# Attention with bias, a gated feed-forward and two adapters: three turned heads in even groups, Gelus of two half batches together, fewer transfers through DRAM copies

## The chip, the core and the metric

The kernel runs on one core of a Trainium2 chip. A core has a matrix engine (TensorE, "PE" in the profile; its weight loads are listed apart as "PEld"), a vector engine (VectorE, DVE), a scalar engine for activation functions (ScalarE, ACT), a general engine (GpSimd, POOL), and SyncE (SP), whose queue issues the transfers of this kernel. Sixteen DMA engines carry the transfers out. On-chip data lie in 128 partitions; TensorE writes to eight PSUM banks.

The metric is device time in microseconds (us) of one execution, as the median of several. The kernel before takes 891.4 us (three runs, 889.95 to 893.95).

## The reference, cut to what matters

Eight batch entries of 512 tokens by 256 features pass an attention block with 16 heads of 16 features and a bias for every head, query and key (8 x 16 x 512 x 512 floats, 134 MB), then a feed-forward block, an adapter whose inner matrix is chosen by a token per batch entry, a rotation, and a second adapter of the same form.

```python
emb = silu(_sin_emb(timestep)) @ W_ada + b_ada
scale, shift = split(emb[:, None, :], 2)
x = _ln(src) * (1.0 + scale) + shift
q, k, v = heads(x @ Wq + bq), heads(x @ Wk + bk), heads(x @ Wv + bv)
scores = einsum('bhqd,bhkd->bhqk', q / sqrt(16), k) + attention_bias
probs = softmax(where(src_mask, -inf, scores))
x = x + (einsum('bhqk,bhkd->bhqd', probs, v) @ Wo + bo)
h = _ln(x) * g2 + beta2
x = x + _gelu2(h @ W1 + b1) @ W2 + b2          # _gelu2(x) = x * sigmoid(1.702 x)
# adapter, twice (before and after the rotation of groups of four features)
hidden = gelu(x @ down_W.T + down_b)
hidden = hidden @ expert_W[idx].T + expert_b[idx] + domain_emb[idx]
x = _ln(hidden @ up_W.T + up_b + x) * ln_gamma + ln_beta
```

## The kernel before

**Steps.** The attention of a batch entry is cut into 16 steps: two halves of 256 queries, four groups g of four heads, and in each two query tiles of 128 (i = 0 and 1). There are 128 steps in all, numbered n. In `attention`, a step loads four bias tiles of 128 x 512 (line 918), one per head j; POOL adds the mask (922); PE computes the four score tiles (930); DVE adds scores to bias and keeps the row's extreme (942); ACT takes the exponential (946). The probabilities then lie with queries on the partitions and have to be turned so that keys do. There are two ways to do that:

- Heads from `turned` on: PE transposes four blocks of 128 x 128 into a PSUM bank (981), and ACT or DVE copies the bank into the tile `pT` (`evict`, 702).
- Heads below `turned`: DVE transposes blocks of 32 x 32 into the tile `tb` (957), and four DMAs, on SP's queue, carry the blocks to their places in `pT` (966). These heads use the values in another order of rows, `v_turn`, which `prepare` makes out of `v_pad` by four DMAs (876).

`turned` is `TURNED = 2` in every group, but in batch 0 in its last group alone. After the second tile of a group come the value products (1007), a small transpose, the division by the sum of the row (1020 to 1036).

**Around it.** `prepare(b)` loads and normalises the next batch entry and makes queries, keys and values; its work is spread over the steps of the batch before. `finish(b, ts)` follows each half batch: output projection (`token_tiles`, 768), `feed_forward` (1061, 1070, 1073, 1077, 1086), then `adapter` twice, l = 0 and 1, then the store of the result (1196). `adapter` transposes the tokens (744, 702), multiplies by the down weight (1116), takes the Gelu on ACT (1124), multiplies by the expert's product with the up weight (768), adds (1133) and normalises. ACT holds one set of functions at a time: between the exponential (946) and the Gelu (1124) the profile shows ACT_TABLE_LOAD.

**At the start.** `late_weights` loads the weights that are needed after the first steps; `wo`, the output weight, comes in eight DMAs, as the host's array has 16 empty rows in each 32 (582). `experts_matrices` fetches, for each batch entry, the chosen expert's matrix of both adapters: SP reads the index into a register and issues two DMAs (1227, 1231).

**What sets the order.** Every piece of work is a task with the engine, a cost in us, what it reads and writes, and a rank. `Plan.run` runs through a model of the engines with these costs, and takes on each engine the ready task of lowest rank whose buffers are free (`Slots`: 15 bias tiles, three `tb`, two `pT`, four `res`, four PSUM banks for scores and four for the rest). `Plan.end` spreads the ranks of a stream (`finish` from n + 2 to n + 11); `Plan.stir` adds small random amounts to ranks, from a list of seeds. The result is a fixed order of instructions per engine; each engine and SP's queue run it in order and wait by semaphores. A transfer waits at SP for its buffer; everything behind it on SP waits too.

Of the kernel before, what the change touches and what calls it, by code (L numbers as in the profile page):

```python
# [20 lines left out]
P = 128  # L21
B, S, D, H, HD, FF = 8, 512, 256, 16, 16, 1024
NT = S // P
# [7 lines left out]
TURNED = 2  # L31
# [49 lines left out]
class Plan:  # L81
# [3 lines left out]
    AFTER = {PE: 0.22, DVE: 0.14, ACT: 0.16, POOL: 0.12, DMA: 2.2}  # L85
# [70 lines left out]
    def run(self, free_at):  # L156
# [13 lines left out]
        landed = [self.BACKLOG + 1.5] * self.FLIGHT  # L170
        while events:
# [15 lines left out]
            for e in [e for e in free_at if e in idle]:  # L187
# [33 lines left out]
                if e == DMA:  # L221
                    begun = now
                    for _ in range(t.many):
                        begun = max(begun, landed[-self.FLIGHT]) + cost / t.many
                        queues = max(queues, begun) + t.data / t.many
                        landed.append(queues + 1.5)
# [22 lines left out]
def conditioned_sequence_kernel(  # L249
# [24 lines left out]
    small = ctx.enter_context(tc.tile_pool(name="small", bufs=1))  # L274
# [8 lines left out]
    def slots(name, count, shape, dtype=F32):  # L283
        return Slots([const.tile(shape, dtype, tag=f"{name}{i}", name=f"{name}{i}") for i in range(count)])

# [13 lines left out]
    BIAS = slots("bias", 15, [P, S])  # L299
    LOW = slots("low", 4, [P, 4])  # L300
    PT = slots("pT", 2, [P, 4 * NT * 2 * P])
    TB = slots("tb", 3, [P, TURNED * S])
# [9 lines left out]
    ST = slots("st", 4, [P, 6])  # L312
    MV = slots("mv", 4, [P, NT, 2])
    RSTD = slots("rstd", 3, [P, 2, NT])
    MINUS = slots("minus", 2, [P, NT])
# [64 lines left out]
    def turned_groups(b):  # L380

        return (NG - 1 if b == 0 else 0), NG
# [23 lines left out]
    turned_rows = tc.dram_tile([B, D], F32, name="turned_rows")  # L406

    def embedding():

        tokf = small.tile([1, 2 * B], F32, tag="tokf", name="tokf")  # L410
        red = small.tile([P, B + 2], F32, tag="red", name="red")
        clip = small.tile([A, B], F32, tag="clip", name="clip")
# [8 lines left out]
        for i in range(42):  # L421
# [4 lines left out]
        plan(DVE, 0.2, lambda: nc.vector.tensor_copy(tokf, tok_i), [], ["tokf"], at=3.2)  # L426
        plan(PE, 0.3, lambda: nc.tensor.matmul(
            scr.t[:, 0, : 2 * B], ones, tokf, start=True, stop=True), ["tokf"], [scr],
            mode="full")

        def reduced():
            turns, last = scr.t[:, 2, : B + 2], scr.t[:, 3, : B + 2]
            nc.vector.tensor_scalar(
# [9 lines left out]
        plan(DVE, 1.2, reduced, [], [scr], at=4.0)  # L443
# [17 lines left out]
        def chosen():  # L461
            domf = scr.t[:A, 0, B : 2 * B]
# [5 lines left out]
        plan(DVE, 0.6, chosen, [], [scr, "valid", "expert"])  # L468
# [101 lines left out]
    def late_weights():  # L570
        wo_rows = w_o.rearrange("(c u j e) n -> c j u e n", c=NC, u=2, e=32)

        def load(rank, cost, data, emit, key, many=1):
# [7 lines left out]
        load(3.0, 3.6, 1.0, lambda: [  # L581
            nc.sync.dma_start(wo[32 * j : 32 * j + 32, c], wo_rows[c, j, :, :HD])
# [840 lines left out]
```

## Time and profile before

| What | us |
|---|---|
| median of three runs | 891.4 (889.95 to 893.95) |
| the profiled execution, its own time | 890.14 |
| its span on the core | 888.4 |
| PE busy | 860.4 (97%) |
| DVE busy | 783.0 (88%) |
| POOL busy | 775.3 (87%) |
| ACT busy | 740.7 (83%) |
| DMA, mean over 16 engines | 78.0% of the span, 217.22 MB on SP's queue |
| TensorE's granted clock, mean | 0.989 |

The page names, for each group of instructions, the line, the engine, the operation, the tiles, the shape and the count; after the bar the busy time in us and the mean ns of one, and after the next bar the idle time of the engine just before these instructions, with what ended most of it. "PE" rows are matmuls, "PEld" rows weight loads. A table by stretches gives each engine's busy time between two moments, counted from the start of the span, then the granted clock (1.00 is full speed), the share of the DMA engines and GB/s. In the list of waits a row reads: who, at which line, waited for which work, in total, how often, and the longest.

### The profile page before, as it was taken

To read this page: it belongs to the slowest core of one execution; us is meant where nothing else is said; L and a number is where in the kernel's file an instruction comes from. 1 tells how busy PE (TensorE), PEld (TensorE's weight loads), DVE (VectorE), ACT (ScalarE), POOL (GpSimd) and SP (SyncE) were. 2 spreads that over 40 slices of the span, in tenths; PEclk is the share of its full clock that TensorE was granted. 3 is DMA by queue.
4 is the path that set the end of the run, shared out by engine and by line. 5 is a ranking of instruction groups with operands and counts; after the bars stand their busy time and mean duration, and the time that the engine had idled before them with its cause. 6 is when DMAs were issued, how large, how long until landed. Compare 5 with 4: busy or idle time off the path is not lost.

```text
span 888.4 us, 20406 instructions
## 1 busy us (share of the span) xinstructions
PE 860.4 (97%) x6430; PEld 565.8 (64%) x6430; DVE 783.0 (88%) x2141; ACT 740.7 (83%) x1349; POOL 775.3 (87%) x907
## 2 busy tenths in 40 slices
PE   9998999999999999999999999999999999999994
PEld 7654675666666666656666666666666566666683
DVE  4757799989999999988998999899999999999766
ACT  5974779979898998979988897988979789799653
POOL 8867999999899898999889997998899999999432
PEclk9998999999999999999999999999999999999997
DMA  9577887698986988888896978968897898998400
GB/s 319 156 226 229 281 254 227 205 293 246 288 276 203 314 276 271 295 243 247 250 317 206 282 238 266 318 202 287 242 309 236 267 284 260 297 298 276 107 25 24
DMA packets 163214, 218.54 MB, mean 246 GB/s; under 512 B 19167, under 2 KB 93961, under 8 KB 163106
## 3 DMA queue, kind: packets, MB, share of 16 engines
q1 hardware_dynamic: 163062, 217.22, 78.0%
q8 instruction: 51, 0.84, 0.4%
q14 instruction: 57, 0.47, 0.2%
q10 hardware_dynamic: 44, 0.02, 0.0%
HBM read 149.89 MB, written 4.24 MB: 173 GB/s over the span
## 4 chain that ended last, share of the span: by engine, by line
PE 56%; ACT 14%; DVE 10%; DMA 8%; POOL 7%; issue 3%; SPq 2%; POOLq 0%; DVEq 0%; ACTq 0%
PE bank L1086 10%; PE bank L930 9%; PE bank L981 8%; PE bank L1061 7%; PE bank L1007 7%; POOL bias L922 5%; DMA bias<-in_bias 5%; ACT bias L946 5%; PE bank L820 4%; DVE bias L942 3%; PE bank L768 3%; ACT pT L702 2%; PE bank L744 2%; PE bank L858 2%; PE bank L419 1%
## 5 line engine op out<-in xcount | busy, mean ns | idle before, releaser
L922 POOL TENSOR_TENSOR bias<-bias,neg 128x512 f32<-128x512 f32 x512 | 580.3, 1161 | 42.3 <-DMA bias<-in_bias 28.2
L946 ACT ACTIVATE bias<-bias,low 128x512 f32<-128x512 f32 x512 | 343.6, 721 | 46.2 <-DVE low L942 45.6
L942 DVE CUSTOM_DVE_ANT_0 bias<-bank,bias 128x512 f32<-128x512 f32 x512 | 328.4, 679 | 42.7 <-PE bank L930 31.4
L981 PEld LDWEIGHTS bank<-shifted,bias 128*128 128x128 f32 x1120 | 124.9, 141 | 77.8 <-ACT bias L946 20.3
L981 PE MATMUL bank<-shifted,bias 128*128 128x128 f32 x1120 | 158.2, 279 | 7.8 <-ACT bias L946 3.2
L957 DVE STREAM_TRANSPOSE tb<-bias 128x512 f32<-128x512 f32 x232 | 155.6, 693 | 4.5 <-ACT bias L946 3.9
L702 ACT COPY pT<-bank 128x512 f32<-128x512 f32 x226 | 125.5, 584 | 35.9 <-PE bank L981 34.1
L930 PE MATMUL bank<-kT,qz 32*128 32x512 f32 x1024 | 149.4, 645 | 0.0
L1007 PE MATMUL bank<-pT,v_pad 128*32 128x256 f32 x1120 | 126.0, 386 | 0.9 <-ACT bias L946 0.9
L1061 PE MATMUL bank<-hT,w 128*128 128x256 f32 (+1 forms) x544 | 125.1, 373 | 1.1 <-ACT hT L754 0.6
L1086 PE MATMUL bank<-w,gT 128*128 128x256 f32 x496 | 119.5, 384 | 0.0
L1007 PE MATMUL bank<-pT,v_turn 128*32 128x256 f32 x928 | 113.1, 386 | 2.0 <-DMA pT<-tb 0.8
L1061 PEld LDWEIGHTS bank<-hT,w 128*128 128x128 f32 x544 | 94.8, 190 | 23.2 <-issue 4.2
L1086 PEld LDWEIGHTS bank<-w,gT 128*128 128x128 f32 x496 | 89.9, 190 | 23.9 <-issue 12.6
L1007 PEld LDWEIGHTS bank<-pT,v_turn 128*32 128x32 f32 x928 | 50.3, 110 | 51.3 <-issue 10.3
L930 PEld LDWEIGHTS bank<-kT,qz 32*128 32x128 f32 x1024 | 42.0, 185 | 42.3 <-issue 27.6
L1070 ACT ACTIVATE sig<-bank,b1s 128x256 f32<-128x256 f32 (+1 forms) x136 | 55.3, 456 | 10.0 <-PE bank L1061 7.2
L1007 PEld LDWEIGHTS bank<-pT,v_pad 128*32 128x32 f32 x1120 | 55.6, 110 | 7.2 <-issue 2.2
L1073 POOL TENSOR_SCALAR sig<-sig 128x512 f32<-128x512 f32 (+1 forms) x68 | 40.1, 593 | 21.8 <-ACT sig L1070 15.8
L1077 DVE SCALAR_TENSOR_TENSOR gT<-bank,cols,sig 128x256 f32<-128x256 f32 (+1 forms) x128 | 54.0, 464 | 4.6 <-POOL sig L1073 4.4
L710 DVE BATCH_NORM_STATS2 st<-res 128x6 f32<-128x256 f32 x128 | 51.4, 410 | 1.7
L718 POOL TENSOR_TENSOR rstd<-rstd,neg_half 128x2 f32<-128x2 f32 (+2 forms) x59 | 43.4, 735 | 4.9
(138 smaller groups left out, 1103.0 us busy)
## 6 DMA issues: line engine op xcount, KB each, us to landing
bias<-in_bias SPq DMA_DIRECT2D x512, 256.0 KB
pT<-tb SPq DMA_DIRECT2D x464, 128.0 KB
out<-res SPq DMA_DIRECT2D x15, 256.0 KB
res<-in_x SPq DMA_DIRECT2D x7, 512.0 KB
v_turn<-v_pad SPq DMA_DIRECT2D x32, 68.0 KB
m<-in_mask SPq DMA_DIRECT2D x8, 256.0 KB
mod<-ada_rows SPq DMA_DIRECT2D x8, 256.0 KB
w<-in_w SPq DMA_DIRECT2D x2, 1024.0 KB
```

The source lines that it names most:

```text
L702: nc.scalar.copy(*pair()) if e == ACT else nc.vector.tensor_copy(*pair())), r, w)
L922: plan(POOL, 1.12, lambda j=j: nc.gpsimd.tensor_tensor(dif[j].t, dif[j].t, negs[qt].t, ALU.add), [negs[qt]], [dif[j]])
L930: nc.tensor.matmul(sc[j].t, qz.t[strip, par, c, qs], kT.t[strip, c, :], start=True, stop=True,)
L942: plan(DVE, 0.61, lambda j=j: nc.vector.tensor_tensor_reduce(dif[j].t, sc[j].t, dif[j].t, -1.0, 3.0e38, ALU.add, ALU.min, low.t[:, j : j + ...
L946: plan(ACT, 0.61, lambda j=j: nc.scalar.activation(dif[j].t, dif[j].t, AF.Exp, bias=low.t[:, j : j + 1], scale=-1.0), [(low, j)], [dif[j]] ...
L957: plan(DVE, 0.62, lambda j=j: nc.vector.transpose(tb.t.rearrange("p (m h k c) -> h p k m c", m=4, h=TURNED, k=NT)[j], dif[j].t.rearrange(" ...
L981: nc.tensor.transpose(ps.t[:, kc, :], dif[j].t[:, kc * P : (kc + 1) * P], ident)
L1007: nc.tensor.matmul(pv.t[32 * j : 32 * j + 32, :], (v_turn if j < turned else v_pad).t[:, at : at + 32], pj, start=(kc == 0), stop=(kc == N ...
L1061: nc.tensor.matmul(ps.t[:, i, :w], w1[:, c, f * P : (f + 1) * P], hT.t[:, c, :w], start=(c == 0), stop=(c == NC - 1),)
L1070: plan(ACT, 0.155 + 0.1 * n, lambda i=i, f=f, ps=ps, sg=sg: nc.scalar.activation(sg.t[:, i, :w], ps.t[:, i, :w], AF.Tanh, bias=b1s[:, f : ...
L1077: plan(DVE, 0.14 + 0.13 * n, lambda i=i, f=f, ps=ps, sg=sg: nc.vector.scalar_tensor_tensor(gT.t[:, f, :w], ps.t[:, i, :w], cols[:, C_B1 + ...
L1086: nc.tensor.matmul(ps.t[:, i, :], gT.t[:, f, i * P : (i + 1) * P], w2[:, f, :], start=(f == 0), stop=(f == NF - 1),)
```

## The change

In groups with even g three of the four heads are turned by DVE and DMA, in the others two as before; batch 0 turns two heads in its last group alone, as before. `tb`, `v_turn` and the moves follow the number. The bias tiles become 14 and `tb` two; small tiles are packed into common ones, and three tiles of the start take a corner of `gT`.

The adapter is split into `way_down` (up to the product before the Gelu) and `way_up` (the rest). The second adapter of a half batch is put off to the `finish` of the next half batch, where its Gelus stand together with those of that half batch's first adapter, in one task of ACT (`gelus`); the last streams run theirs at once. The store goes with the second adapter.

The output weight is copied within DRAM into a dense array by two DMAs and loaded by one; both adapters' experts are copied into one array by two DMAs, the eight indices are read into registers at once, and each batch entry's two matrices come by one DMA. The turned values are written to DRAM in one DMA and read back in the other order in one.

Costs in the planner's model are altered, and its list of seeds is another one (21 rows before, 36 after).

```diff
-TURNED = 2
+TURNED = 3
...
-    AFTER = {PE: 0.22, DVE: 0.14, ACT: 0.16, POOL: 0.12, DMA: 2.2}
+    AFTER = {PE: 0.22, DVE: 0.14, ACT: 0.16, POOL: 0.12, DMA: 2.45}
...
-        landed = [self.BACKLOG + 1.5] * self.FLIGHT
+        landed = [self.BACKLOG + 2.0] * self.FLIGHT
...
+    def packed(name, count, shape):
+        t = const.tile([P, count, *shape[1:]], F32, tag=name, name=name)
+        return Slots([t[:, i] for i in range(count)])
...
-    BIAS = slots("bias", 15, [P, S])
-    LOW = slots("low", 4, [P, 4])
+    BIAS = slots("bias", 14, [P, S])
+    LOW = packed("low", 4, [P, 4])
     PT = slots("pT", 2, [P, 4 * NT * 2 * P])
-    TB = slots("tb", 3, [P, TURNED * S])
+    TB = slots("tb", 2, [P, TURNED * S])
...
-    ST = slots("st", 4, [P, 6])
-    MV = slots("mv", 4, [P, NT, 2])
-    RSTD = slots("rstd", 3, [P, 2, NT])
-    MINUS = slots("minus", 2, [P, NT])
+    ST = packed("st", 4, [P, 6])
+    MV = packed("mv", 4, [P, NT, 2])
+    RSTD = packed("rstd", 3, [P, 2, NT])
+    MINUS = packed("minus", 2, [P, NT])
...
-    def turned_groups(b):
-
-        return (NG - 1 if b == 0 else 0), NG
+    def turned_heads(b, g):
+
+        if b == 0 and g < NG - 1:
+            return 0
+        return TURNED if g % 2 == 0 else TURNED - 1
...
+    both = tc.dram_tile([2, E, A * AW], F32, name="both")
+    TURNED_SIZE = NT * NG * TURNED * (HD + 1)
+    value_rows = [tc.dram_tile([P, TURNED_SIZE], F32, name=f"value_rows{i}") for i in range(2)]
+    wo_dense = tc.dram_tile([NC, P, D], F32, name="wo_dense")
...
-        wo_rows = w_o.rearrange("(c u j e) n -> c j u e n", c=NC, u=2, e=32)
+        wo_rows = w_o.rearrange("(c u j e) n -> u c j (e n)", c=NC, u=2, e=32)
+        rows = wo_dense.rearrange("c (j u d) n -> u c j (d n)", u=2, d=HD)
...
-        load(3.0, 3.6, 1.0, lambda: [
-            nc.sync.dma_start(wo[32 * j : 32 * j + 32, c], wo_rows[c, j, :, :HD])
-            for c in range(NC) for j in range(4)
-        ], "wo", many=8)
+        plan.rank = 2.4
+        plan(DMA, 1.1, lambda: [
+            nc.sync.dma_start(rows[u], wo_rows[u, :, :, : HD * D]) for u in range(2)
+        ], [], ["wo_dense"], data=0.8, many=2)
+        plan.rank = 3.0
+        plan(DMA, 0.5, lambda: nc.sync.dma_start(
+            wo, wo_dense.rearrange("c p n -> p c n")), ["wo_dense"], ["wo"], data=0.8)
...
-        def turned_values():
-            size = NT * NG * TURNED * (HD + 1)
-            to = v_turn.t.rearrange("(r m) f -> m r f", m=4)
-            for m in range(4):
-                nc.sync.dma_start(to[m, :, :size], v_pad.t[32 * m : 32 * m + 32, :size])
-
-        plan(DMA, 2.6, turned_values, [(v_pad, t) for t in range(NT)], [v_turn], data=1.0, many=4)
+        rows = value_rows[b % 2]
+        plan(DMA, 0.5, lambda: nc.sync.dma_start(rows, v_pad.t[:, :TURNED_SIZE]),
+             [(v_pad, t) for t in range(NT)], [("values", b % 2)], data=0.4)
+        plan(DMA, 0.5, lambda: nc.sync.dma_start(
+            v_turn.t[:, :TURNED_SIZE], rows.rearrange("(m r) f -> r m f", m=4)),
+            [("values", b % 2)], [v_turn], data=0.6)
...
-        turned = TURNED if g in range(*turned_groups(b)) else 0
+        turned = turned_heads(b, g)
...
-                tb.t.rearrange("p (m h k c) -> h p k m c", m=4, h=TURNED, k=NT)[j],
+                tb.t[:, : turned * S].rearrange("p (m h k c) -> h p k m c", m=4, h=turned, k=NT)[j],
...
-            run = TURNED * P
+            run = turned * P
             to = pT.t[:, : 8 * run].rearrange("p (a q f) -> a q p f", a=4, q=2)
             for a in range(4):
                 nc.sync.dma_start(
-                    to[a, i], tb.t[32 * a : 32 * a + 32].rearrange("r (m f) -> r m f", m=4)
+                    to[a, i], tb.t[32 * a : 32 * a + 32, : turned * S].rearrange("r (m f) -> r m f", m=4)
...
-                 data=1.05 * TURNED, many=4)
+                 data=0.8 * turned, many=4)
...
-    eus, rots = {}, {}
-
-    def adapter(b, l, res, rk, ts):
-        n, w = len(ts), len(ts) * P
-        rows = slice(ts[0], ts[0] + n)
+    eus, rots, late = {}, {}, []
+
+    def way_down(b, l, res, rk, ts):
+        n = len(ts)
         if ts[0] == 0:
 
             ps, eu = Buffer(BG, lambda t: t[:A1, :D]), Buffer(EU)
@@ -1104,11 +1115,9 @@
                 ps.t, ewT[l][: A1 + 1 + 7 * l, b, :], wu[: A1 + 1 + 7 * l, l, :], start=True,
                 stop=True), [("ewT", l), "wu", *rk], [ps], mode="full")
             evict(lambda ps=ps: (eu.t, ps.t), [ps], [eu], 0.35, 0.35)
-            eus[l] = eu
-        eu = eus[l]
+            eus[b, l] = eu
         xT, xk = half_transposed(lambda t: res.t[:, t, :], rk, ts)
         ps, hid = Buffer(BG, lambda t: t[:, :P]), Buffer(HID)
-
 
         def down():
             for c in range(NC):
@@ -1118,6 +1127,8 @@
                         start=(c == 0), stop=(c == NC - 1),
                     )
 
+        plan(PE, 0.52, down, [*xk, "wd"], [ps], mode="down")
+
         def hidden():
             for i in range(n):
                 lanes = slice(A * i, A * i + A)
@@ -1126,8 +1137,21 @@
                     bias=db[lanes, b : b + 1] if l else db[lanes, B:],
                 )
 
-        plan(PE, 0.52, down, [*xk, "wd"], [ps], mode="down")
-        plan(ACT, 0.27 * n, hidden, [ps, "hid1", "db"], [hid], mode="gelu")
+        return b, l, res, rk, ts, ps, hid, hidden
+
+    def gelus(ways):
+
+        def hidden():
+            for way in ways:
+                way[-1]()
+
+        plan(ACT, 0.27 * sum(len(way[4]) for way in ways), hidden,
+             [*(way[5] for way in ways), "hid1", "db"], [way[6] for way in ways], mode="gelu")
+
+    def way_up(b, l, res, rk, ts, _, hid, hidden):
+        n = len(ts)
+        rows = slice(ts[0], ts[0] + n)
+        eu = eus[b, l]
...
+            plan(DMA, 0.42, lambda: nc.sync.dma_start(
+                out[b].rearrange("(t p) d -> p t d", p=P)[:, rows], res.t[:, rows]), rk, [],
+                data=0.4 * len(ts))
...
-    def finish(b, ts, store=None):
+    def finish(b, ts, store=None, last=False):
...
-        adapter(b, 0, res, rk, ts)
-        adapter(b, 1, res, rk, ts)
-        plan(DMA, 0.42, lambda: nc.sync.dma_start(
-            out[b].rearrange("(t p) d -> p t d", p=P)[:, rows], res.t[:, rows]), rk, [],
-            data=0.4 * len(ts))
+        ways = [way_down(*way) for way in late]
+        late.clear()
+        ways.append(way_down(b, 0, res, rk, ts))
+        gelus(ways)
+        for way in reversed(ways):
+            way_up(*way)
+        late.append((b, 1, res, rk, ts))
+        if last:
+            way = way_down(*late.pop())
+            gelus([way])
+            way_up(*way)
...
+        plan.rank = 2.2
+        plan(DMA, 1.1, lambda: [
+            nc.sync.dma_start(both[l], experts[l].rearrange("(e p) a -> e (p a)", e=E))
+            for l in range(2)
+        ], [], ["both"], data=1.8, many=2)
+        chosen = []
+        plan.rank = 2.6
+        plan(DMA, 0.8, lambda: chosen.extend(nc.values_load_multi_w_load_instructions(
+            expert_i, engines=[EG.SP], min_val=0, max_val=E - 1)[1]), ["expert"], ["chosen"])
         for b in range(B):
             plan.rank = 2.7 + 0.55 * b
-
-            def fetch(b=b):
-                e = nc.sync.value_load(
-                    expert_i[:, b : b + 1], min_val=0, max_val=E - 1,
-                )
-                for l in range(2):
-                    nc.sync.dma_start(
-                        raw.t[:, l, b, :],
-                        experts[l].rearrange("(e p) a -> e p a", e=E)[bass.ds(e, 1)].rearrange(
-                            "o p a -> (o p) a"),
-                    )
-
-            plan(DMA, 2.0, fetch, ["expert"], [(raw, b)], data=0.2, many=2)
+            plan(DMA, 0.75, lambda b=b: nc.sync.dma_start(
+                raw.t[:, :, b, :],
+                both[:, bass.ds(chosen[b], 1)].rearrange("l o (p a) -> p (l o) a", a=AW)),
+                ["both", "chosen"], [(raw, b)], data=0.3)
...
-                finish(u[0], [2 * half, 2 * half + 1])
+                finish(u[0], [2 * half, 2 * half + 1], last=n > 110)
...
             for t in range(2):
                 plan.begin()
                 finish(u[0], [2 + t], Buffer(PT, lambda p: p.rearrange(
-                    "p (c q) -> p c q", q=2 * P)[:, :NF]) if t else None)
+                    "p (c q) -> p c q", q=2 * P)[:, :NF]) if t else None, t == 1)
                 plan.end(n + 2.0 + 4 * t, n + 11.0 + 4 * t)
     plan.stir([
-        (410212, 1.8, 6.8, 0.15),
-        (199711, 113.2, 123.2, 0.5),
...
+        (263804, -99.0, 9999.0, 0.15),
+        (944984, -99.0, 9999.0, 0.15),
+        (106075, 108.8, 118.8, 0.15),
...
```

## The prediction

> **What bounds the kernel now.** I read the page's busy shares, then busy time by stretches of one batch, then the groups of instructions, then who waits for whom. The stretches come first: the seven between 113 and 834 us are the steady state, one batch each (the 1,024 score matmuls of L930, eight per step, put 101.4, 103.1, 103.7, 105.8, 101.8 and 97.8 us between the starts of batches 1 to 7). Columns: us, then busy time of PE, PEld, DVE, ACT, POOL, then granted clock, DMA share, GB/s.
>
> ```profile
> 113.00:216.00 103.00, 101.24 (x749) 66.18 (x746) 95.59 (x260) 89.69 (x161) 100.38 (x111) 1.00 0.82 254
> 319.00:422.00 103.00, 101.79 (x768) 65.90 (x765) 94.38 (x260) 91.33 (x163) 95.86 (x110) 1.00 0.85 264
> 628.00:731.00 103.00, 102.12 (x768) 65.81 (x768) 96.76 (x259) 89.31 (x159) 95.36 (x106) 1.00 0.86 263
> 834.00:888.40 54.40, 42.84 (x296) 33.53 (x288) 35.09 (x99) 24.13 (x65) 17.79 (x44) 0.91 0.10 31
> ```
>
> Over the seven stretches PE averages 101.7 of 103, DVE 96.5, POOL 95.4, ACT 91.1, and DMA runs at a share of 0.85. PE is the bound with 1.3 us lost per batch, and three others stand close behind. The groups price what the change touches; the last two columns are mean ns and idle time before.
>
> ```profile
> L981 PE MATMUL bank<-shifted,bias 128*128 128x128 f32 x1120 | 158.2, 279 | 7.8 <-ACT bias L946 3.2
> L957 DVE STREAM_TRANSPOSE tb<-bias 128x512 f32<-128x512 f32 x232 | 155.6, 693 | 4.5 <-ACT bias L946 3.9
> L702 ACT COPY pT<-bank 128x512 f32<-128x512 f32 x226 | 125.5, 584 | 35.9 <-PE bank L981 34.1
> L702 DVE COPY pT<-bank 128x512 f32<-128x512 f32 x54 | 35.9, 676 | 4.8 <-PE bank L981 4.5
> L946 ACT ACT_TABLE_LOAD x27 | 34.6, 1283 | 0.5
> L1124 ACT ACT_TABLE_LOAD x27 | 34.6, 1283 | 0.4
> ```
>
> Who waits says where DVE's slack goes and how the loads stand.
>
> ```profile
> DVE bias L942 <- PE bank L930: 31.4, 32, 5.1
> POOL bias L922 <- DMA bias<-in_bias: 28.2, 26, 3.0
> SPq L918 <- PE bank L981: 74.5, 51, 8.4
> SPq L918 <- DVE tb L957: 25.3, 20, 5.0
> SPq L918 <- ACT bias L946: 21.6, 60, 1.3
> ```
>
> DVE's longest wait is for PE, so a lighter PE also relieves DVE. SP waits 121 us for a free bias tile, and 28.2 us of late loads reach POOL.
>
> **Part by part. Turned heads.** The built program has 896 transposes on PE at L981 where 1,120 stood: 56 blocks of four gone, 8 in each of batches 1 to 7 (batch 0 keeps two heads in its last group and none elsewhere). In the timeline a block begins at 412.56 and the next matmul at 413.09, 0.53 us. Bounds: the 28 in a row of the chain took 3.33 us, so 0.48 a block; the group's 158.2 us / 280 is 0.57. I take 0.53, 4.2 us of PE per batch, 30 in all (27 to 32). The value matmuls only change their weight tile (L1007 386 ns from either).
>
> With these blocks go 56 evictions: on ACT 226 to 192, on DVE 54 to 32. DVE gains 56 transposes, 56 x 0.693 = 38.8 us. The built order also gives ACT work that DVE had: 13 hT copies, 9 eu, 2 xT. So DVE loses 22 x 0.676 + 13 x 0.681 + 9 x 0.414 + 2 x 0.795 = 29.0 and nets +9.8, about 1.3 per batch: 97.8.
>
> The steady state then has PE at 97.5, DVE at 97.8, POOL at 95.4. If DVE loses the 1.3 that PE loses now, a batch takes 99.1 (gain 3.9). If DVE keeps its present 6.5 of idle, it takes 104.3 (loss 1.3). I take 100.1, nearer the lower end, because most of DVE's idle time is spent on PE's results (31.4 at L942, 8.6 at L1020, 6.7 at L1133) and PE becomes shorter; but two engines tied cannot both be fed without gaps. Gain 2.9 x 7 = **-20 us** (-27 to +9).
>
> **Gelu pairs.** 27 loads of the Gelu table and 27 back become 14 and 14: 26 x 1.283 = 33.4 us off ACT. With 34 x 0.584 fewer evictions and 13 x 0.584 + 9 x 0.364 + 2 x 0.771 more copies, ACT loses 41 us, 5.4 per batch. ACT is not the bound, so I cost this at nothing beyond the smoother feed already taken. Cover: PE's 97.5. The joint Gelu on ACT must wait for the later of two `down` products; exponentials and evictions are queued behind it, and PE's transposes wait for those. One such wait now is "ACT hid L1124" for "PE bank L1116", 3.4 us in five. The second adapter of a half batch is moved eight steps later with all it issues (two transposes per tile, statistics, POOL's power, norm, the store, on SP past some 32 bias loads). Nothing waits for that store; its `res` tile is freed about eight steps later, and the fourth tile is needed only some 14 steps after that. The Trainium skill, "ScalarE: Activation LUTs", section "What ACT_TABLE_LOAD costs", gives 2.66 us per switch, load plus drain; the trace has a load at 403.65 for 1.28 us and its Gelu at 404.95, so no drain shows. By the page ACT would lose 26 x 2.66 = 69 us instead of 33, still off the bound.
>
> **Transfers.** 224 of the 464 moves `pT<-tb` grow from 128 to 192 KB: +14.7 MB, same count and issue time on SP. The turned values go to DRAM and back (two DMAs of 408 KB a batch for 272 KB in four): +4.5 MB. At the page's 217.22 MB for a 78.0% share of 888.4 us, 3.19 us per MB, that is 61 us, 8 per batch: 87.4 becomes 95.4. The low bound is nothing, if the row count decides, since the rows only lengthen. I take 95 of 100.1: just hidden, at a share of 0.95. The read of the turned values waits on SP for the write to land; eight bias loads stand between the two in batch 1's order, and the first values that use it run 40 us after the old transfer was issued (43.45 against 85.9), so 0.
>
> **Fewer buffers.** 15 bias tiles become 14, three tb become two. A tile turns over in 15 x 1.61 = 24.1 us now and would in 14 x 1.56 = 21.9. DVE waited once for a tb, 0.4 us, and a step is 6.4 us, so two tb give 12.9 us for transposes, four issues (2.5 us) and landing. I take 0 for both; the other end is a rival below.
>
> **Start.** Between 55 and 105 us SP is the limit while PE starves.
>
> ```profile
> 37.85 5.49 SPq L582 DMA_DIRECT2D wo<-in_w_o  x8
> 43.45 2.77 SPq L876 DMA_DIRECT2D v_turn<-v_pad  x4
> 73.80 1.23 SPq L1231 DMA_DIRECT2D gT<-in_experts  x2
> 80.00:85.00 5.00, 1.76 (x17) 1.20 (x15) 3.85 (x10) 1.44 (x2) 3.98 (x4) 0.84 0.88 277
> 85.00:90.00 5.00, 5.00 (x40) 2.48 (x44) 1.55 (x5) 1.82 (x3) 5.00 (x6) 0.50 0.97 344
> ```
>
> Eight fetches at 1.13 to 1.39 (9.8 us) plus about 0.78 each for loading the register (6.2) become two copies, one load and eight issues of 0.6: -7. Output weight 5.5 to 1.5: -4. Turned values of two batches 5.2 to 1.8: -3. So some 14 us of SP go. PE idles 6.1 us there and loses 5 more at half clock, 11 at most to win; DMA shares of 0.88 to 0.97 say that part is data, not issue. I take **-4** (-11 to +2).
>
> **Tail.** Of the last tokens one tile's second adapter now runs beside the other's chain: on DVE 0.41 + 0.41 + 0.18 + 0.85 = 1.9 us, and a moved adapter of batch 6 brings 3.2 more, with DVE busy 35.1 of 54.4. **+1** (-1 to +4).
>
> Sum: 888.4 - 20 - 4 + 1 = 865; with the 1.7 us that lie around the span (890.14 - 888.4), **867**. The profiled run stands 1.3 us under the median of three; that is inside their spread.
>
> A rule against: the Trainium skill, "Perfetto Trace Analysis", section "Identifying the Most-Contended Engine", says that matmul busy time misjudges TensorE's headroom and to use weight-load busy time, here 64%. By it PE is not the bound and the removed blocks pay nothing: -3 alone, 887. The stretches above, with matmuls waiting 1.3 us in 103, decide for me.
>
> **Rivals.** (a) *DVE takes PE's place in full*: it is within 0.3 us of PE after the change. For it: 93.7% busy now. Against: its waits are on PE. A batch at 102 gives -7 - 4 + 1: 880. (b) *The tie costs nothing and the start recovers*: 99.1 a batch, -27, start -9, tail +1: 855. For it: ACT's 5.4 us freed in front of PE. (c) *DMA becomes the bound, slower*: place, the bias loads of batches 1 to 7; work 95.4 us per batch. If the queues hold no more than 0.90, a batch takes 106, +21 - 4 + 1: 908. It decides below a sustained share of 95.4 / 103 = 0.93. For it: POOL already waits 28.2 us for loads, and one tile fewer. Against: 1.07 was held from 12 to 20 us, 0.93 to 0.97 from 85 to 95. (d) *No change*: the edits do not do what they say. The instruction counts exclude it, leaving a balance of gains and waits near 891.
>
> **How the numbers follow.** Forecast 0.55, (a) 0.17, (b) 0.13, (c) 0.11, (d) 0.04. The time is the forecast's, 867. Half of (b) and most of (c) lie outside 850 to 887, 0.17 in all. Half a per cent, 4.5 us, is about what these measurements can tell: faster 0.85, same 0.04, slower 0.11.
>
> **What would show it.** Stretches of about 100 us per batch with PE and DVE both near 98 and DMA at 0.95; 896 transposes at L981's place; 28 table loads; POOL's wait for bias loads not above some 40 us; no PE idle of 3 us near 80. I am wrong if POOL's or DVE's wait for loads doubles, or if PE's idle time per batch grows past 5 us.

## The result: 1.3% slower

The changed kernel takes 901.6 us (median of eight runs, 896.8 to 905.4) against 890.7 for the kernel before (eight runs, 887.2 to 894.0): a ratio of 1.0128, 95% interval 1.0101 to 1.0155. The prediction was 867 us, faster. The profiled execution took 904.15 us, 2.6 above the median; its span is 902.4.

Where the time went is seen first from three moments in each trace: the first score matmul of batch 1, the first of the last step, and the end. The columns are the stretches between them, in us; "run" is the median of the runs, so that the three stretches, which come from one profiled execution, need not add up to it. The experiments told of below stand in the same table.

| Kernel | to batch 1 | batch 1 to last step | tail | run |
|---|---|---|---|---|
| before | 127.9 | 700.4 | 60.1 | 890.7 |
| changed | 119.0 | 719.6 | 63.7 | 901.6 |
| changed, two of three turned heads moved | 118.2 | 698.0 | 62.0 | 879.7 |
| changed, third turned head free | 119.6 | 692.9 | 61.9 | 875.5 |
| changed, bias loads cut to 3/4 | 117.8 | 711.2 | 62.7 | 887.9 |
| before, PE lighter by 22 us | 127.6 | 699.4 | 60.4 | 890.4 |
| before, DVE heavier by 38 us | 126.2 | 715.3 | 60.4 | 905.5 |

The start gained 8.9 us, the tail lost 3.6, and the batches lost 19.2 where the prediction had gained 20.

The same stretches of 103 us in the profile of the changed kernel (us, then busy time of PE, PEld, DVE, ACT, POOL, granted clock, DMA share, GB/s):

```profile
216.00:319.00 103.00, 97.06 (x712) 60.90 (x711) 90.77 (x248) 83.68 (x152) 90.26 (x102) 0.98 0.90 279
525.00:628.00 103.00, 100.67 (x740) 64.24 (x740) 94.59 (x262) 87.16 (x160) 95.03 (x109) 1.00 0.93 289
628.00:731.00 103.00, 97.13 (x718) 61.23 (x716) 93.69 (x250) 83.77 (x153) 92.04 (x104) 0.97 0.91 282
```

Over the seven stretches every engine is less busy than before (PE 98.1 where it was 101.7, DVE 93.6 after 96.5, POOL 93.4 after 95.4, ACT 83.9 after 91.1); only DMA has risen, from 0.85 to 0.87 in the first stretch and 0.90 to 0.93 in the other six. No engine is nearer to full than it was: they wait. The groups say that the edits did what they say, and the waits say for what (who, at which line, for which work, total, times, longest):

```profile
L993 PE MATMUL bank<-shifted,bias 128*128 128x128 f32 x896 | 131.2, 280 | 7.3 <-ACT bias L958 5.6
L969 DVE STREAM_TRANSPOSE tb<-bias 128x512 f32<-128x512 f32 x288 | 191.5, 689 | 20.7 <-DMA pT<-tb 17.1
L715 ACT COPY pT<-bank 128x512 f32<-128x512 f32 x192 | 108.6, 581 | 45.7 <-PE bank L993 45.0
L1135 ACT ACT_TABLE_LOAD x14 | 18.0, 1283 | 0.2
```

```profile
POOL bias L934 <- DMA bias<-in_bias: 50.6, 54, 3.5
DVE tb L969 <- DMA pT<-tb: 17.1, 15, 3.2
PE bank L1019 <- DMA pT<-tb: 10.8, 7, 2.0
PE bank L1019 <- DMA bias<-in_bias: 4.9, 2, 3.3
```

The same waits for the moves in the kernel before:

```profile
DVE tb L957 <- DMA pT<-tb: 0.4, 1, 0.4
PE bank L1007 <- DMA pT<-tb: 0.8, 1, 0.8
```

POOL's wait for late bias loads rose from 28.2 us to 50.6; DVE's wait for a `tb` whose moves had not landed from 0.4 to 17.1; the value products' wait for the moves from 0.8 to 10.8. SP shows it too: the durations of its issue instructions, summed from the trace, rose from 227 to 261 us for the 512 bias loads and from 289 to 322 for the 464 moves, with the same counts. In a three-head step the fourth move's issue takes 1.14 us (median of 56), in a two-head step 0.61 (median of 60).

What comes late costs PE twice, by the wait and by the clock. Between the first score of batch 1 and the last step it stood idle for 34.0 us, before for 8.8 (summed from the traces); ten of the gaps lasted 1.6 to 3.3 us, where the kernel before has none over 1.5. And within 1.2 us of the end of six of them the granted clock stood at 0.50 for 3.4 us, 20.5 us in all, while the kernel before keeps full speed all through its batches. At half clock that is 10 us of PE's work at the most (an estimate). It is not the whole loss: the two of the eight runs with the highest mean clock, 0.989 as in the kernel before, still took 896.8 and 897.6 us.

The start, in the timeline of SP's queue of the changed kernel (begin and length in us, then the transfer):

```profile
42.66 1.45 SPq L593 DMA_DIRECT2D wo_dense<-in_w_o  x2
47.09 0.56 SPq L888 DMA_DIRECT2D v_turn<-value_rows  x1
52.42 0.39 SPq L596 DMA_DIRECT2D wo<-wo_dense  x1
54.11 2.07 SPq L1267 DMA_DIRECT2D gT<-both  x2
```

The last of the eight expert fetches (L1267) is issued at 64.8 us, against 73.8 before. Two stretches of 5 us of the same kernel, with the columns of the stretches above:

```profile
80.00:85.00 5.00, 4.90 (x48) 2.96 (x41) 3.65 (x10) 2.63 (x6) 5.00 (x6) 1.00 0.90 298
85.00:90.00 5.00, 5.00 (x53) 3.12 (x46) 4.55 (x15) 2.31 (x5) 5.00 (x6) 1.00 1.02 364
```

PE, which stood idle for 3.2 us between 80 and 85 us and then ran at half clock, is busy and at full clock there.

### The profile page after: what moved, and what is told of

The parts are those of the page before. It is cut to its first block, busy times and chain, and to the rows that moved or that the text cites. A ratio compares the mean times of both kernels' runs of the same rounds, so it can differ in the third digit from the quotient of the medians.

```text
span 902.4 us, 19763 instructions
## 1 busy us (share of the span) xinstructions
PE 850.5 (94%) x6206; PEld 549.7 (61%) x6206; DVE 785.5 (87%) x2152; ACT 707.3 (78%) x1312; POOL 775.4 (86%) x907
## 3 DMA queue, kind: packets, MB, share of 16 engines
q1 hardware_dynamic: 163786, 237.16, 84.4%
## 4 chain that ended last, share of the span: by engine, by line
PE 46%; DVE 13%; DMA 13%; POOL 10%; ACT 10%; issue 5%; SPq 3%; DVEq 0%; POOLq 0%; ACTq 0%
PE bank L1019 8%; PE bank L942 8%; PE bank L1073 6%; PE bank L1098 6%; POOL bias L934 6%; PE bank L993 6%; DMA bias<-in_bias 6%; DMA pT<-tb 6%; DVE bias L954 5%; PE bank L833 3%; ACT bias L958 3%; DVE tb L969 3%; SPq L978 2%; PE bank L781 2%; PE bank L757 2%
## 5 line engine op out<-in xcount | busy, mean ns | idle before, releaser
L934 POOL TENSOR_TENSOR bias<-bias,neg 128x512 f32<-128x512 f32 x512 | 581.3, 1160 | 58.0 <-DMA bias<-in_bias 50.6
L958 ACT ACTIVATE bias<-bias,low 128x512 f32<-128x512 f32 x512 | 341.9, 717 | 62.7 <-DVE low L954 61.8
L969 DVE STREAM_TRANSPOSE tb<-bias 128x512 f32<-128x512 f32 x288 | 191.5, 689 | 20.7 <-DMA pT<-tb 17.1
L942 PE MATMUL bank<-kT,qz 32*128 32x512 f32 x1024 | 154.3, 642 | 0.1
L993 PEld LDWEIGHTS bank<-shifted,bias 128*128 128x128 f32 x896 | 100.3, 141 | 78.0 <-ACT bias L958 33.7
L715 ACT COPY pT<-bank 128x512 f32<-128x512 f32 x192 | 108.6, 581 | 45.7 <-PE bank L993 45.0
L993 PE MATMUL bank<-shifted,bias 128*128 128x128 f32 x896 | 131.2, 280 | 7.3 <-ACT bias L958 5.6
L1019 PE MATMUL bank<-pT,v_turn 128*32 128x256 f32 x1152 | 118.0, 400 | 16.0 <-DMA pT<-tb 10.8
L1019 PE MATMUL bank<-pT,v_pad 128*32 128x256 f32 x896 | 129.2, 393 | 0.7 <-ACT pT L715 0.7
L1098 PE MATMUL bank<-w,gT 128*128 128x256 f32 x496 | 119.0, 382 | 0.1
L1019 PEld LDWEIGHTS bank<-pT,v_turn 128*32 128x32 f32 x1152 | 55.3, 113 | 69.0 <-issue 23.7
L942 PEld LDWEIGHTS bank<-kT,qz 32*128 32x128 f32 x1024 | 45.0, 184 | 44.4 <-issue 25.3
L1085 POOL TENSOR_SCALAR sig<-sig 128x512 f32<-128x512 f32 (+1 forms) x68 | 40.2, 593 | 14.7 <-ACT sig L1082 10.6
L745 ACT ACTIVATE bank<-res,rstd 128x256 f32<-128x256 f32 x64 | 36.2, 566 | 14.6 <-POOL rstd L732 13.6
```

The source lines that it names most:

```text
L715: nc.scalar.copy(*pair()) if e == ACT else nc.vector.tensor_copy(*pair())), r, w)
L934: plan(POOL, 1.12, lambda j=j: nc.gpsimd.tensor_tensor(dif[j].t, dif[j].t, negs[qt].t, ALU.add), [negs[qt]], [dif[j]])
L942: nc.tensor.matmul(sc[j].t, qz.t[strip, par, c, qs], kT.t[strip, c, :], start=True, stop=True,)
L958: plan(ACT, 0.61, lambda j=j: nc.scalar.activation(dif[j].t, dif[j].t, AF.Exp, bias=low.t[:, j : j + 1], scale=-1.0), [(low, j)], [dif[j]] ...
L969: plan(DVE, 0.62, lambda j=j: nc.vector.transpose(tb.t[:, : turned * S].rearrange("p (m h k c) -> h p k m c", m=4, h=turned, k=NT)[j], dif ...
L993: nc.tensor.transpose(ps.t[:, kc, :], dif[j].t[:, kc * P : (kc + 1) * P], ident)
```

## Experiments

Theory A says that the third head's transfers and the fewer buffers cost; B that the Gelus of two half batches together do; C that the list of seeds picked a bad order.

### Seeds, heads and pairs

```diff
-    plan.stir([
...
-    ])
```

> The kernel before with its list of seeds left empty, so that ranks are as the code sets them. It is the base for three of the next runs. If the order that the seeds pick is worth much (theory C), about 905 to 915 us; if it is worth little, 890 to 898.

Measured: 900.1 us, ratio to the kernel before 1.012 (1.009 to 1.0149): between the two expectations.

> The changed kernel with an empty list of seeds. Theory A (the parts of the change itself cost, by transfers and fewer buffers) and theory B (the Gelus of two half batches together cost): slower than the kernel before without seeds, by about as much as now, 8 to 15 us. Theory C (the parts are good, the new seeds picked a bad order for this chip): not slower than the kernel before without seeds, and by my forecast's sum up to 20 us faster.

Measured: 914.1 us, ratio 1.0284 (1.025 to 1.0318). The seeds are worth 10 us in the one kernel and 12.5 in the other. Theory C falls: without seeds the changed kernel stands 14 us behind, with them 11.

```diff
-TURNED = 3
+TURNED = 2
...
-        return TURNED if g % 2 == 0 else TURNED - 1
+        return TURNED
...
-    BIAS = slots("bias", 14, [P, S])
+    BIAS = slots("bias", 15, [P, S])
...
-    TB = slots("tb", 2, [P, TURNED * S])
+    TB = slots("tb", 3, [P, TURNED * S])
```

> The changed kernel without seeds, two turned heads in every group as before, with 15 bias tiles and three tb as before. Theory A: 15 to 25 us faster than the changed kernel without seeds, DVE's wait for tb's transfers near 0 again and POOL's wait for bias loads back near 30 us from 50. Theory B: within 5 us of it. My forecast's own terms: 20 us slower than it.

Measured: 900.65 us, ratio 1.0122 (1.0069 to 1.0176), 13.5 us faster than three heads without seeds; POOL's wait for loads is 28.8 us, DVE's for tb 0.4. That is A's side, just short of its 15 us; heads, bias tiles and tb are set back together here.

```diff
         late.append((b, 1, res, rk, ts))
-        if last:
+        if True:
```

> The changed kernel without seeds, each half batch running its second adapter at once as before, 27 Gelu table loads again. Theory B: 10 to 20 us faster than the changed kernel without seeds, and the long step in the second half of each batch (11 to 15 us now) gone. Theory A: within 5 us of it, or slower, since ACT takes up 33 us of table loads again.

Measured: 934.6 us (926.5 to 940.8), ratio 1.0527 (1.0478 to 1.0575), some 20 us slower. Theory B, which said 10 to 20 faster, falls. These four kernels are each planned anew, and an order alone can be worth 10 us, as the seeds are; the next four runs keep the changed kernel's order.

### What of the third head costs

```diff
                 nc.sync.dma_start(
-                    to[a, i], tb.t[32 * a : 32 * a + 32, : turned * S].rearrange("r (m f) -> r m f", m=4)
+                    to[a, i, :, : 2 * P],
+                    tb.t[32 * a : 32 * a + 32, : turned * S].rearrange(
+                        "r (m f) -> r m f", m=4)[:, :, : 2 * P],
                 )
```

> The changed kernel in its own order, but in even groups the four moves carry two of the three turned heads: 128 KB instead of 192 KB, 14.7 MB less, the third head's probabilities left as pT holds them. Every other instruction and wait stays. If the bytes of the moves are what delays the loads (theory A, transfers), it is 12 to 20 us faster than the changed kernel and POOL's wait for bias loads falls from 51 to about 30 us. If the number of tb tiles or the order decides, within 5 us of it.

Measured: 879.7 us, ratio 0.9887 (0.9869 to 0.9905): 22 us faster than the changed kernel, a little more than A's 12 to 20, and 10 faster than the kernel before; it leaves the third head's part of `pT` old. The order, every semaphore wait in the program and every other instruction are the changed kernel's. What the waits cost in its profile:

```profile
POOL bias L934 <- DMA bias<-in_bias: 25.7, 30, 2.9
DVE tb L969 <- DMA pT<-tb: 7.2, 6, 2.2
```

The issue instructions on SP are back at 234 us for the loads and 295 for the moves.

```diff
+    MOD, ROT = Slots([rows2]), Slots([rows2])
+    bv_row, wd = rows2[:, 0], wv[:, 0].rearrange("p (l c a) -> p l c a", l=2, c=NC)
...
-        plan(DMA, 0.4, lambda: nc.sync.dma_start(
-            mod.t.rearrange("p r d -> p (r d)"), ada_rows[b].partition_broadcast(P)),
+        plan(DMA, 0.4, lambda: None,
```

> Control for the next run. The changed kernel in its own order, but the per-batch rows for the modulation and the rotation, the value bias and the down weight are not loaded; other tiles stand in for them, so that 6 KB a partition come free, and 16 transfers of 256 KB and two small ones are left out (4.2 MB of 237). Theory A, transfers: about 4 us faster than the changed kernel, in proportion to the bytes (61 us of DMA work per 19 MB, a third of which reaches the end). Otherwise within 2 us.

Measured: 900.4 us, ratio 1.0122 (1.0076 to 1.0169). Within 2 us of the changed kernel, the second side: 4.2 MB less of these loads makes no difference that shows.

```diff
-    TB = slots("tb", 2, [P, TURNED * S])
+    TB = slots("tb", 3, [P, TURNED * S])
+    TB.free = [0, 1]
...
+    respread(TB, 3)
```

Here `respread` runs after the plan and hands the tiles, longest free first, to the buffers in the order they have.

> As the control, but the tb buffers take turns on three tiles instead of two; order, bytes and every other buffer are the same. If the wait for a free tb is a cause (theory A, buffers): DVE's 17 us of waiting for tb's transfers goes to about 0 and the time falls by 8 to 17 us against the control. If those waits only stand in for late loads: within 3 us of it.

Measured: 901.3 us, ratio 1.0142 (1.0115 to 1.0169), against 900.4 for the control. DVE's wait for tb is gone from the list, and two others have grown:

```profile
POOL bias L930 <- DMA bias<-in_bias: 48.0, 52, 3.4
PE bank L1015 <- DMA pT<-tb: 12.5, 8, 4.1
```

In the control they were 38.6 and 7.6. A third tb tile, in an order planned for two, moves the waiting to other engines and is worth nothing; the 17 us of DVE's waits were not a price to be added up.

```diff
+            cut = S if n < 4 else 3 * P
-                dif[j].t, bias[b, 4 * g + j, qt * P : (qt + 1) * P, :]), [], [dif[j]], data=0.84)
+                dif[j].t[:, :cut], bias[b, 4 * g + j, qt * P : (qt + 1) * P, :cut]),
```

> The changed kernel in its own order, but from the fifth step on each bias load brings 384 of its 512 columns, 32.5 MB less in all; the moves carry all they should. This asks where the order would end if transfers were never late. If transfers are all that my sum missed, about 865 us (my forecast), with POOL's wait for loads under 15 us and few held issues on SP. If they are only the part that the third head's bytes showed (22 us), 875 to 882, and the engines' coupling or the order holds the rest.

Measured: 887.9 us, ratio 0.9964 (0.9937 to 0.999), 14 us faster than the changed kernel. That is 6 us above the expected 875 to 882. Its lines say more, though the profiled execution, 893.4 us, was the longest of ten. The page has SP's queue with its packets, bytes in MB and share of the DMA engines:

```profile
q1 hardware_dynamic: 163786, 204.65, 78.8%
```

Among its waits, POOL's for the bias loads:

```profile
POOL bias L936 <- DMA bias<-in_bias: 34.8, 34, 2.9
```

SP's queue carries 12.6 MB less than in the kernel before, at its share of the DMA engines. Still the issues take 268 us for the loads and 316 for the moves, as in the changed kernel, the fourth move of a three-head step 1.03, POOL waits longer for loads than before, and the batches take 711 us. So the total of bytes and the mean share don't explain the delay by themselves: 14.7 MB off the moves give 22 us, 32.5 MB off the loads 14.

```diff
             for a in range(4):
...
+            if b and g % 2 == 0:
+                nc.sync.dma_start(spill[i], tb.t[:, :S])
```

> The kernel before in its own order, and in each step of an even group of batches 1 to 7 one more transfer, 256 KB from tb out to DRAM that nobody reads: 56 of them, 14.7 MB, what the third head adds to the moves. If bytes by themselves cost what they cost in the changed kernel, 10 to 20 us slower than the kernel before, and SP's issues held longer (49 us over their median now, 107 in the changed kernel). If it takes the shorter period and fewer buffers of the changed kernel for them to bite, 0 to 5 us.

Measured: 919.1 us, ratio 1.0322 (1.0283 to 1.0361), 29 us slower, beyond both. But not by the way that was asked about: the issues are not held (220 and 284 us), and what grew is SP's wait for an earlier transfer to land:

```profile
SPq L919 <- DMA bias<-in_bias: 24.2, 64, 2.3
```

It was 9.7 us in 27 waits. POOL's wait for loads rose with it, from 28.2 to 49.8 us, nearly as far as in the changed kernel. These are 56 transfers more in the queue, out to DRAM; the run says how little room SP's order has, not what the moves' bytes cost.

```diff
             for a in range(4):
-                nc.sync.dma_start(
+                held.append(lambda a=a: nc.sync.dma_start(
...
+        for n, move in enumerate(held):
+            if n < 2:
+                move()
+            else:
+                waiting.append([due, n - 1, move])
```

> The changed kernel; of each step's four moves the third is issued behind the next bias load and the fourth behind the one after it, where the values that need them come later than that. Bytes, counts and all other orders stay. In the changed kernel the fourth move of a three-head step is held at SP for 1.14 us, against 0.61 for a two-head step. If it is the burst of four that holds SP and makes the bias loads behind it late, the fourth move's issue falls to about 0.6 us and the time by 5 to 15 us. If the queues' work as a whole is what is late, or moves now wait behind loads that wait for a free tile, 0 to 10 us slower.

Measured: 946.9 us, ratio 1.0586 (1.0552 to 1.062). 45 us slower than the changed kernel, far past what either side expected. The profiled execution was the longest of the four, 955.75 us, so its lines are only rough. In them DVE's wait for a `tb` rose to 39.7 us and the value products' wait for moves to 38.9: it is the moves that come late now. The fourth move's issue did fall to 0.61 us, but the third's, behind a bias load, rose to 1.06 (medians of 56), and SP's issues took 269 us for the loads and 312 for the moves, 581 together where the changed kernel has 583. So parting the four moves only shifted the hold, as far as this profile shows.

### Is PE the bound, or DVE?

```diff
             def turn(j=j, ps=ps):
-                for kc in range(NT):
+                for kc in range(1 if b and g % 2 == 0 and j == 2 else NT):
```

> The kernel before in its own order; in even groups of batches 1 to 7 one of the heads turned by PE gets one of its four transposes, so 168 fewer, 22 us of PE at 0.13 each, and what is read of the rest of the bank is old. My forecast's step (PE is the bound, the other engines follow within 2.4 us a batch) says 12 to 20 us faster. If PE's 99% is mostly time in which it is handed work as fast as the others make it, 0 to 6 us.

Measured: 890.4 us, ratio 0.9983 (0.9965 to 1.0001): 1.6 us of the 22 taken from PE, on the side of 0 to 6. The page's line of engines:

```profile
PE 851.2 (96%) x6262; PEld 548.6 (62%) x6262; DVE 782.7 (88%) x2141; ACT 741.7 (84%) x1349; POOL 775.0 (87%) x907
```

A stretch of 103 us of the same run:

```profile
319.00:422.00 103.00, 100.40 (x741) 63.48 (x739) 93.24 (x258) 90.28 (x163) 94.66 (x108) 1.00 0.84 262
```

PE still counts as busy for 100.4 us of 103, with 24 transposes fewer in it; over the whole kernel its busy time fell by 9 us, not 22. So a busy share near one did not mean here that the end follows PE's work. The evictions of these blocks stayed, and POOL, the third of the close engines, was not tried in this way.

```diff
-            plan(DVE, 0.62, lambda j=j: nc.vector.transpose(
+            plan(DVE, 0.62, lambda j=j: [nc.vector.transpose(
...
+                for _ in range(2 if b and g % 2 == 0 and j == 1 else 1)], [dif[j]], [(tb, j)])
```

> The kernel before in its own order; in even groups of batches 1 to 7 DVE does one of its two transposes twice, 56 more, 35 to 39 us of DVE, nothing else. My forecast's step took DVE's own growth (10 us net of evictions) as covered by its 6.5 us of idle time a batch: by it, 0 to 6 us slower. If DVE is as much the bound as PE, 20 to 35 us slower, half a microsecond for each.

Measured: 905.5 us, ratio 1.0155 (1.0137 to 1.0173), 13.4 us slower: 0.24 us for each of 56 transposes of 0.69. Between the two expectations.

```profile
PE 865.5 (96%) x6430; PEld 565.7 (63%) x6430; DVE 816.8 (91%) x2197; ACT 743.9 (82%) x1349; POOL 777.1 (86%) x907
```

DVE's busy time rose by 34 us, of which somewhat over a third came through.

```diff
-            plan(DVE, 0.62, lambda j=j: nc.vector.transpose(
+            plan(DVE, 0.62, lambda j=j: j < 2 and nc.vector.transpose(
...
+                    to[a, i, :, : 2 * P],
...
```

> The changed kernel in its own order; in even groups the third turned head is neither transposed by DVE nor carried by the moves (its probabilities stay what pT holds), so that PE's 30 us and the evictions are saved and nothing is paid for them. With the third head's bytes alone left out it took 879.7. If the third head's transposes on DVE cost here what 56 transposes cost in the kernel before (13 us), 865 to 869, about my forecast: then the change's saving is there and DVE and the moves cost 35 us. If DVE has slack once the bytes are gone, 876 to 880, and the order or the fewer bias tiles hold the rest.

Measured: 875.5 us, ratio 0.9812 (0.9774 to 0.985); 4 us faster than with the bytes alone left out, 6 when each is set against the kernel before in its own session (891.6 and 889.7), and just below the second side's 876. With the third head costing nothing, on DVE or in the queues, the changed kernel still stands 8 us above the forecast.

```profile
319.00:422.00 103.00, 100.71 (x753) 65.21 (x752) 92.12 (x252) 89.48 (x165) 98.25 (x113) 1.00 0.89 274
```

DVE has come down to 92 us of 103; PE still counts 100.7.

### The other parts alone

The first run took the three kinds of copies into the kernel before, seeds and all; the second has the pairs without the rest, with the old transfers; the third only the copies for the output weight and the experts; the fourth the same with a list of seeds of its own.

```diff
-        load(3.0, 3.6, 1.0, lambda: [
...
+        plan(DMA, 0.5, lambda: nc.sync.dma_start(
+            wo, wo_dense.rearrange("c p n -> p c n")), ["wo_dense"], ["wo"], data=0.8)
```

> The kernel before, with only the output weight, the experts and the turned values by copies in DRAM. In the two profiles batch 1's first scores came at 119.0 us against 127.9. If the copies give that, 4 to 9 us faster than the kernel before; if the double path of the turned values costs later (4.5 MB more in all), the gain is lost again, within 3 us; a re-drawn order can move it by some us either way.

Measured: 904.9 us, ratio 1.0166 (1.0149 to 1.0183). That is 15 us slower than the kernel before, where 4 to 9 faster or no more than 3 off was expected. Batch 1 begins at 120.3 us, as hoped, but the batches take 724.4. The old seeds fall on other tasks here, so that the 10 us they are worth may be gone too; that would leave 5, and their cause isn't shown.

```diff
-        rows = value_rows[b % 2]
...
+        def turned_values():
...
-TURNED = 3
+TURNED = 2
```

> Without seeds: Gelus of two half batches together, two turned heads, the old transfers, 15 bias tiles and three tb. Against the kernel before without seeds (900.1) it shows the pairs alone, against the run with two heads and the new transfers (900.7) the transfers alone. If pairs are good where three heads are turned (914 against 935 without them) and good here too, 885 to 893, and the copies cost 8 to 15 us. If pairs matter only under three heads, about 900.

Measured: 910.65 us, ratio 1.022 (1.017 to 1.0271): 10 us slower than the kernel before without seeds, neither of the two expected; and 10 slower than the same with the copies. So the pairs, worth some 20 us under three heads, cost 10 here. Each of these orders is planned anew, and orders of the same parts differ by 10 us with their seeds, so what pairs and copies are worth by themselves isn't settled.

```diff
-            nc.sync.dma_start(wo[32 * j : 32 * j + 32, c], wo_rows[c, j, :, :HD])
...
+            nc.sync.dma_start(rows[u], wo_rows[u, :, :, : HD * D]) for u in range(2)
...
+            nc.sync.dma_start(both[l], experts[l].rearrange("(e p) a -> e (p a)", e=E))
```

> The kernel before without seeds, with the copies for the output weight and the experts only; the turned values go by the four old transfers. If the start's gain (batch 1 at 118 to 120 us instead of 126 to 128) is that of these two and nothing is paid later, 890 to 893 against 900.1. If the whole gain is given back in the batches, 898 to 902.

Measured: 897.2 us, ratio 1.0069 (1.004 to 1.0098), 3 us faster than without seeds and copies, just below the second side; batch 1 at 120.6, the batches 711.6 against 706.7 (there the profile caught the fastest of four).

```diff
+    plan.stir([
+        (136758, 77.4, 82.4, 0.5),
...
+    ])
```

> The kernel before with the copies for the output weight and the experts only (897.2 without seeds) and a list of seeds of its own, drawn anew and kept where the planner's order ends earlier. If seeds are worth the 10 us here that they are worth in the kernel before, 885 to 889, faster than both kernels. If a new draw is worth nothing on the chip, about 897.

Measured: 890.9 us (12 runs), ratio 0.9987 (0.997 to 1.0004). The seeds are worth 6 us here. Batch 1 begins at 120.1 and the batches take 707.8 against 700.4: the start's 8 us are given back. It is level with the kernel before; no version that computes the whole result beat that one.

## Why the prediction was wrong

**"PE is the bound with 1.3 us lost per batch."** This step failed first. Of the 30 us saved on PE, 20 were booked as gain, as PE's busy time was taken for the time that the batches need. Taking 22 us of the same transposes out of the kernel before gave 1.6. The rule that the prediction set aside, of the Trainium skill, "Perfetto Trace Analysis", section "Identifying the Most-Contended Engine", spoke for the right side: matmul busy time said 99%, weight-load busy time 64%, and PE's work was not what set the time. By that rule the prediction's own sum came to 887; what was left out of that sum is the next step.

**"I take 95 of 100.1: just hidden."** The second step. The transfers' volume was priced rightly (237.16 MB and 84.4% of the span, 69 us more DMA work by these shares where 61 were worked out), and the share came to 0.90 to 0.93. That it would be hidden was wrong: the third head's bytes cost 22 us. Rival (c) named the place, late bias loads, and came nearest with 908; POOL's wait for loads, whose doubling was named as a sign of being wrong, rose by four fifths. But its rule (a sustained share under 0.93 decides) isn't what the runs show: with three quarters of the bias loads the share over the span was the old one, and the moves were still held and late (DVE waited 12.7 us for them).

**"If DVE keeps its present 6.5 of idle."** A size. DVE's net growth of 10 us was taken into the 2.3 us that DVE was to lose per batch. 38 us of added transposes cost 13.4 in the kernel before, so 10 would cost some 3.5 (an estimate in proportion); the third head's 39 us of transposes cost 4 to 6 in the changed kernel's order, once the bytes were gone.

**"Gain 2.9 x 7 = -20 us."** With nothing paid for the third head, the batches gained 7.5 us (700.4 to 692.9). That is what PE's 30 us, 56 evictions and 26 table loads were worth together, in this order and with fewer bias tiles. With its transposes 2.4; with its bytes too, minus 19.2. So of the 39 us by which the batches miss the forecast, the bytes make 21.6, DVE's transposes 5.1, and 12.5 are saving on PE and ACT that never reached the end (one profile of each kernel).

**Fewer buffers, 0 for both.** Right for the third tb: no gain with three. The fifteenth bias tile wasn't tried alone.

**Start, -4 (bounds -11 to +2).** Right in kind, mis-sized: -8.9 in the profiles, most of the 11 us of PE's idle and half-clock time. Whether it reaches the end isn't shown: in the kernel before with copies and seeds of its own the batches gave back 7.4 of 7.8. All thirteen kernels with the copies begin batch 1 between 117 and 121 us, the six without between 124 and 129.

**Tail, +1 (-1 to +4).** It measured +3.6, inside.

**Gelu pairs, nothing.** Table loads fell from 27 to 14 each as counted, and ACT from 740.7 to 707.3 us. Under three heads the pairs are worth some 20 us, under two heads -10, each against a newly planned order; so the term of nothing is neither shown nor refuted.

How the larger moves make SP's issues longer isn't shown; only that they do (583 us for loads and moves against 516), that it goes with their bytes (529 without the third head's), that it hardly goes with the bias loads' (583 with three quarters of them), and that a bias load between the moves doesn't end it (581, in the rough profile).

## What to carry to other kernels

Here four engines and the queues were each busy for 78 to 97% of the time, and the busiest did not set it: 22 us less work on PE gave 1.6, while 38 us more on DVE cost 13. Before a redesign rests on a busy share, take a slice of work from that engine in the old order and see whether the time follows. On-chip moves weren't free because the number of issues stayed: they stand in the same queue as the loads, and with 14.7 MB more in them the loads behind came late. Waits for a late transfer couldn't be added up as a gain: a third tb tile took DVE's 17 us away, and POOL and PE waited 14 us more.

## What was not expected of the hardware

A transfer of 192 KB between on-chip tiles, 128 rows of 1,536 bytes, held SP's issue for 1.14 us as the fourth in a row, against 0.61 for 128 KB. Its packets took 65 ns in the median, against 46 ns for packets of 1,024 bytes and 84 ns for those of 2,048. 56 transfers of 256 KB out to DRAM, one in each step of every other group, cost 29 us in a kernel whose DMA engines stood at a share of 0.85. And gaps of PE of 1.6 to 3.3 us in the middle of a kernel that is busy throughout were followed by half clock in six cases of ten.
